# Norm transposes a step later, one exchange first in its queue, three regroupings and one pair of banks reordered

## The chip, the cores and the metric

The kernel runs on one core of a Trainium2 chip. The metric is the device time of one execution in microseconds (us), the median over several executions. Five engines work beside each other, each on its own stream of instructions in the order written: PE (TensorE, matrix products), DVE (VectorE), ACT (ScalarE), POOL (GpSimd) and SP (SyncE), which here issues nearly all DMAs. They wait for each other through semaphores. SBUF is the on-chip memory of 128 partitions; PSUM holds the results of matrix products, in eight banks of 2 KB a partition.

## The reference

One transformer block in float32: self-attention, cross-attention to a context, and a gated feed-forward, each behind a layer norm and with a residual. Batch 2, 1024 rows of 256 features, 16 heads of 64, a context of 154 rows of 192 features, 1024 gated features.

```python
h = _layernorm(x, ln1_g, ln1_b)
x = _attention(h, h, sa_wq, sa_wk, sa_wv, sa_wo, sa_bo) + x
h = _layernorm(x, ln2_g, ln2_b)
x = _attention(h, cond_emb, ca_wq, ca_wk, ca_wv, ca_wo, ca_bo) + x
h = _layernorm(x, ln3_g, ln3_b)
p = h @ ff_w1 + ff_b1
a, gate = (p[..., :D_FF], p[..., D_FF:])
h = a * jax.nn.gelu(gate, approximate=False) @ ff_w2 + ff_b2
return h + x
```

## The kernel before

The order of every instruction is written out by hand; no scheduler changes it. All of it is one stream of Python loops that emit instructions for the five engines, and each engine keeps its own.

**Units and steps.** A unit is a batch row and a pair of heads, 16 in all. Self-attention is a loop over 128 steps `p`, eight a unit (a step's slot is `p % 8`). A step computes the scores of 128 rows against all 1024 keys for the two heads (`s`, L497), their maxima on DVE (L681), the exponents on ACT (L508, output `p`), and an exchange of the running maxima and sums between partitions by four DMAs (`st`, L518). POOL turns these into differences (`dd`, L526 and L527) and denominators (L537 and L539), ACT into factors (`ee`, L532), DVE takes reciprocals (`rd`, L609), POOL scales the exponents by them (L619), and DVE transposes them in 32 by 32 blocks (`pT`, L644). In slots 3 and 4, and 7 and 0, PE does the weighted sums with the values (`po`, L549), which begin in slot 3 or 7 and need the transposed weights of four earlier steps; ACT copies them out in the step after (`store` in `self_values`, L666).

**Work beside.** In the other slots `run_work` puts projections beside the scores, for the next unit (`pq_sa`, `pk_sa`, `pv_sa`), output tiles (`py_sa`, L471, added to `x` at L478) and the layer norm that the next stage needs. What such a piece returns, its store, is emitted in the next step, after that step's scores and maxima and ahead of its exponents (`flush(stores)`):

```python
then = self_first(p)
flush(stores)
then()
```

**The norms beside.** `norm_beside` (L331) lays out a norm in small steps: statistics (`stats`, L240), deviation (L246), normalise (an offset on DVE, L256, then two activations on ACT, L274, or on POOL at L271 in the wide form) and turn (`turn`, L284): four transposes of a 128 by 128 tile by PE into one PSUM bank, `ph_ln`, and as store four activations by ACT into `hT_ln` (L299). In the narrow form, which is self-attention's norm of the second batch row and cross-attention's of the first, one row tile is taken per step and the four turns of each norm come in slot 5 of units 3, 4, 5 and 6, and of 11, 12, 13 and 14. Normalise of a later tile pair comes in slot 6.

**Banks.** `mm_tile`, `sum_tile` and the scores each rotate over two buffers in PSUM. The turn's `ph_ln` and the weighted sums' `po` both take `sum_tile`. A tile that takes a buffer waits until the earlier one there has been read.

**SP's queue.** SP issues in order: the four DMAs of each exchange, the weights ahead of their use (`load_ahead`, `load_weights`, L134, L123), and what stands in the list `later`, among it the swaps of the context's values between partitions (`v_ca`, L800) and the copies of their ends (L805).

**Cross-attention and the gated stage.** Cross-attention has 48 steps `c`, three a unit: scores (`sc`, L828), maxima, exponents (L845), scaling (L856), transposes into the ring `pT_ca` (L872). `cross_regroup` (L889) then copies blocks by eight DMAs between partitions into a single tile of pairs (shown as `wf`, whose memory it uses), and `cross_weigh` lets `cross_values` (L908) make the weighted sums `poc` of a unit in two parts: part 0 in two `sum_tile` banks, part 1 in two `mm_tile` banks, each copied out to `o_ca` (L922). Only when both parts of two units are there can the output tiles `py_ca` be made. The last two units' sums, 14 and 15, lie among the first steps of the gated feed-forward (`pa`, `pb`, `pc`, L1029), whose `pa` also takes `mm_tile` banks; there the copies of a part are shared by ACT and DVE (`pools` is set).

Of the kernel before, what the change touches and what calls it, by code (L numbers as in the profile page):

```python
# [18 lines left out]
def tile_transformer_block(ctx: ExitStack, tc: tile.TileContext, a: dict, out: bass.AP):  # L19
# [11 lines left out]
    HP = NPAIR // NQ  # L31
    NT = S // P
# [20 lines left out]
    SH = GH // 2  # L53
# [44 lines left out]
    for n in names:  # L98
        k = n_of[n]
# [39 lines left out]
    def load_weights(kind, pr, what):  # L139
        if kind == "sa" or what == "q":  # L140
            wsl[kind, pr, what] = load_slice(f"{kind}_w{what}", pr * P, P, HR)
        elif pr % 2 == 0:
            wsl[kind, pr, what] = load_slice(f"{kind}_w{what}", pr * P, VC, CC)
# [23 lines left out]
    for n in names[2:]:  # L167
        own = rows[row_of[n] - n_cols:row_of[n] - n_cols + n_of[n], :]
        p = HR if n in twice else P
# [44 lines left out]
    hT, vs, qk, oT = {}, {}, {}, {}  # L214
# [93 lines left out]
    def tile_order(kind):  # L308

        if kind == "ff":  # L310
            return list(range(NT))
        return [t for i in range(NT // 2) for t in (i, NT // 2 + i)]

    def narrow(kind, b):

        return kind == "sa" or kind == "ca" and b < B - 1

    def add_biases(kind, b):

        bo = {"sa": "sa_bo", "ca": "ca_bo", "ff": "ff_b2"}[kind]  # L320

        def add(t):
            xs = xt[b, t // GT][:, t % GT, :]
            nc.gpsimd.tensor_tensor(xs, xs, bias[bo], ALU.add)

        later.extend(lambda t=t: add(t) for t in range(NT))
        if b == B - 1 and kind != "ff":
            later.append(lambda: load_bias({"sa": "ca_bo", "ca": "ff_b2"}[kind]))

    def norm_beside(kind, b):  # L330

        after = {"sa": None, "ca": "sa", "ff": "ca"}[kind]
        stats, deviation, normalize, turn = norm_pieces(kind, b)
        n = 1 if narrow(kind, b) else 2
        lag = {}
        for fns, first in ((turn, 3), (stats, 0), (deviation, 1), (normalize, 2)):
            for i, fn in enumerate(fns):  # L340
                t = i if fns is stats else 2 * i + 1
                lag.setdefault(first + t // n, []).append((fn, fns is turn))
        for k in range(NT // n + 3):
            tiles = tile_order(kind)[k * n:(k + 1) * n]
            needs = [(after, b, half, t) for half in range(NQ) for t in tiles if after]

            def step(fns=lag[k]):
                done = [fn() for fn, _ in fns]
                return next((fn for fn in done if fn), None)

            side.append((any(turns for _, turns in lag[k]), needs, step))
        if not narrow(kind, b):
            side.append((False, (), lambda: add_biases(kind, b)))

# [203 lines left out]
    side, lates = [], []  # L558
    stores, adds = [], []
    later = []  # L560

    def run(piece):
        done = piece()
        if done is not None:
            (adds if getattr(done, "adds", False) else stores).append(done)
# [34 lines left out]
    SA = 2 * SH * NU  # L600
# [113 lines left out]
    def load_ahead(p):  # L714

        ui, n = divmod(p, 2 * SH)
        for what in "qkv":
            at = {"q": 2, "k": 3, "v": 2 * SH - 1}[what] + 3 * (ui == 0 and what != "v")
            if n != at or ui + 2 >= NU and what == "k":
                continue  # L720
            if ui + 2 < NU:
                load_weights("sa", units[ui + 2][1], what)
            elif ui + 2 == NU or what == "q":
                load_weights("ca", units[ui + 2 - NU][1], what)
        if p == SA - 2:
            load_weights("ca", units[2][1], "q")
        if p in (LAG + 1, 2 * SH - 1, SA - SH - 6):
            load_keys(2 * (1 + (LAG + 1, 2 * SH - 1, SA - SH - 6).index(p)), 2)


    CG = [(t, min(TG, NT - t)) for t in range(0, NT, TG)]
    CA = len(CG) * NU
# [144 lines left out]

    def cross_regroup(c):

        ui, n = divmod(c - len(CG) - 2, len(CG))  # L880
        if n != 0 or not 0 <= ui < NU:
            return
        for a2 in range(2):
            for a4 in range(P // KB):
                half, e = divmod(a4, 2)
                own = slice(a4 * KB, (a4 + 1) * KB)
                src = slice((2 * half + a2) * KB, (2 * half + a2 + 1) * KB)
                blocks = pTc["ring"][src, ui % 3, :2 * NM].rearrange("p (m e) j q -> p m e (j q)", e=2)
                nc.sync.dma_start(  # L889
                    out=pTc["pairs"][own, a2].rearrange("p m j q -> p m (j q)"), in_=blocks[:, :, e])  # L890

    def cross_values(ui, a2):

        b, pr = units[ui]
        v, v0 = vs["ca", b, pr // 2], pr % 2 * P
        if a2 == 0 and pr % HP == 0:
            oT["ca", b, pr // HP] = pt_.tile([P, HP, S], F32, tag="oT", name=f"o_ca{b}_{pr}")  # L900
        quarters = (a2, 2 + a2)
        po = {a4: (mm_tile if a2 else sum_tile)(f"poc_{ui}_{a4}") for a4 in quarters}
        for m in range(NM + 1):
            for a4 in quarters:
                r0 = a4 // 2 * QG
                r = slice(r0, r0 + QG)
                for j in range(2):
                    nc.tensor.matmul(  # L908
                        po[a4][j * DH:(j + 1) * DH, :NT * KB],
                        lhsT=v[r, m + a2 * (m == NM), v0 + j * DH:v0 + (j + 1) * DH],  # L910
                        rhs=pTc["pairs"][r, a2, m, j] if m < NM else
                        pTc["ring"][r, ui % 3, NB - 1, j, :],
                        start=(m == 0), stop=(m == NM),
                        tile_position=(r0, j * DH),
                    )
        dst = oT["ca", b, pr // HP][:, pr % HP, :].rearrange(
            "p (t a q) -> p t a q", a=P // KB, q=KB)

        def store():
            for a4 in quarters:  # L920
                copy = nc.scalar.copy if pools and a4 // 2 else nc.vector.tensor_copy
                copy(dst[:, :, a4, :], po[a4][:, :NT * KB].rearrange("p (t q) -> p t q", q=KB))  # L922

        return store
# [18 lines left out]
    def cross_weigh(c):  # L943

        ui, n = divmod(c - 2 * len(CG) - 1, len(CG))
        if n == 0 and 0 <= ui < NU:
            for part in range(2):
                run(lambda: cross_values(ui, part))
            flush(stores)

# [4 lines left out]
    wsum, wh, ub, psum, pools = {}, {}, {}, {}, {}  # L955
# [259 lines left out]
    with tc.manual_schedule():  # L1215
        stats, deviation, normalize, turn = norm_pieces("sa", 0, True)
# [58 lines left out]
        for p in range(SA):  # L1275
            if p % (2 * SH) == 0:
                self_beside(p // (2 * SH))
            if p == SA - SH:
                work.extend(held)
                held.clear()  # L1280
# [3 lines that stand above are left out]
            turn_group(p - LAG - 1, 1)  # L1284
            turn_group(p - LAG, 0)
            if adds:
                adds.pop(0)()
            flush(kept)
            if later and (p < 4 or p % (2 * SH) in (2, 4, 6)):
                later.pop(0)()  # L1290
            if p in ahead:
                ahead[p]()
            load_ahead(p)
            h, hg = divmod(p, SH)
            ui, n = divmod(p, 2 * SH)
            if h and hg == SH - 1:
                run(lambda: self_values(h - 1, 0))
            elif h > 1 and hg == 0:
                run(lambda: self_values(h - 2, 1))
            else:  # L1300
                run_work(2 if p < SA - SH else 1, h % 2 or h == 0, sum_tile)
                if p == LAG:
                    load_weights("sa", units[1][1], "v")
            if hg == LAG:
                f = (ui - NPAIR // 2 - 1) * EC
                if n == LAG and 0 <= f < DA // 2:
                    load_ends(f, min(EC, DA // 2 - f))
                elif n == SH + LAG and 0 <= f < DA // 2:
                    run(lambda: context_ends(f, min(EC, DA // 2 - f), sum_tile))
                if n == SH + LAG and ui in (0, 1, NU - 1):  # L1310

                    pr = {0: 2, 1: 4, NU - 1: 6}[ui]
                    run(lambda: context_keys(pr, sum_tile))
                    kept.append(context_keys(pr + 1, mm_tile))

        for c in range(CA):
# [13 lines left out]
            ui, n = divmod(c, len(CG))  # L1330
# [81 lines left out]
        for k in range(2 * FU):  # L1412
            c = CA + k
# [17 lines left out]
            while n_left > 0 and sums:  # L1431
                fn, n = sums.pop(0)
# [51 lines left out]
```

## Time and profile before

| what | value |
|---|---|
| median of 3 executions | 1082.0 us (1080.7 to 1082.27) |
| the profiled execution | 1079.84 us |
| its span | 1078.0 us |
| granted PE clock | 1.000 of full speed |
| PE busy | 1062.9 us, 99% |
| DVE busy | 887.4 us, 82% |
| POOL busy | 774.9 us, 72% |
| ACT busy | 645.6 us, 60% |
| DMA moved | 60.84 MB, mean 56 GB/s |

The page gives for each engine how long it was busy, and groups of instructions by line, engine and operation, with tile names as output<-input. The waits by engine tell for each kind of instruction what ended the idle time in front of it. A timeline has a row for neighbouring instructions of one kind: start from the span's start, length, engine, line, operation, tiles, shape, and how many instructions the row merges. SPq is SP issuing DMAs. PE's matmuls overlap each other, so rows overlap a little. The chain of work that ended last is 87% PE.

### The profile page before, as it was taken

To read this page: it belongs to the slowest core of one execution; us is meant where nothing else is said; L and a number is where in the kernel's file an instruction comes from. 1 tells how busy PE (TensorE), PEld (TensorE's weight loads), DVE (VectorE), ACT (ScalarE), POOL (GpSimd) and SP (SyncE) were. 2 spreads that over 40 slices of the span, in tenths; PEclk is the share of its full clock that TensorE was granted. 3 is DMA by queue.
4 is the path that set the end of the run, shared out by engine and by line. 5 is a ranking of instruction groups with operands and counts; after the bars stand their busy time and mean duration, and the time that the engine had idled before them with its cause. 6 is when DMAs were issued, how large, how long until landed. Compare 5 with 4: busy or idle time off the path is not lost.

```text
span 1078.0 us, 46825 instructions
## 1 busy us (share of the span) xinstructions
PE 1062.9 (99%) x19300; PEld 697.1 (65%) x19300; DVE 887.4 (82%) x1327; ACT 645.6 (60%) x2068; POOL 774.9 (72%) x1652
## 2 busy tenths in 40 slices
PE   8999999999999999999999999999999999999998
PEld 6556556556565565565665655566766777788998
DVE  5789999998989989999989889968877877655554
ACT  5766766677666657676776666656566554342231
POOL 2677777778777777777777777766756786499884
PEclk9999999999999999999999999999999999999999
DMA  3222122112111121111111101125775545000000
GB/s 91 65 74 49 43 48 53 43 43 50 32 43 31 33 51 34 39 42 29 39 40 26 43 15 37 24 70 146 183 181 126 116 109 120 7 5 16 21 11 30
DMA packets 104726, 60.84 MB, mean 56 GB/s; under 512 B 32378, under 2 KB 95298, under 8 KB 104514
## 3 DMA queue, kind: packets, MB, share of 16 engines
q1 hardware_dynamic: 103138, 57.07, 22.2%
q8 instruction: 152, 2.49, 0.9%
q10 hardware_dynamic: 1376, 0.79, 0.2%
q14 instruction: 60, 0.49, 0.1%
HBM read 27.91 MB, written 2.10 MB: 28 GB/s over the span
## 4 chain that ended last, share of the span: by engine, by line
PE 87%; POOL 3%; DMA 3%; DVE 3%; SPq 2%; issue 1%; ACT 1%; POOLq 0%; DVEq 0%; ACTq 0%
PE s L497 19%; PE po L549 19%; PE py_sa L471 5%; PE py_ca L471 5%; PE pv_sa L397 5%; PE pk_sa L366 4%; PE pq_sa L366 4%; PE pq_ca L366 4%; PE poc L908 4%; PE pb L1029 4%; PE pq L1168 3%; PE sc L828 3%; PE pa L1029 2%; PE pc L1029 2%; SPq L518 2%; DMA st<-st 2%
## 5 line engine op out<-in xcount | busy, mean ns | idle before, releaser
L619 POOL TENSOR_SCALAR p<-p,rd,ee 128x512 f32<-128x512 f32 x512 | 390.4, 768 | 94.0 <-DVE rd L609 91.8
L508 ACT ACTIVATE p<-s,st 128x512 f32<-128x512 f32 x512 | 345.5, 686 | 169.7 <-DVE st L681 164.0
L681 DVE TENSOR_REDUCE st<-s 128x2 f32<-128x1024 f32 x256 | 308.7, 1207 | 55.4 <-issue 17.2
L644 DVE STREAM_TRANSPOSE pT<-p 128x1024 f32<-128x1024 f32 x256 | 302.9, 1220 | 2.4 <-POOL p L619 2.2
L497 PE MATMUL s<-k_sa,q_sa 64*32 64x512 f32 x4096 | 250.5, 591 | 2.7 <-ACT p L508 2.0
L549 PE MATMUL po<-pT,v_sa 64*32 64x256 f32 x8192 | 235.6, 376 | 0.6 <-DVE pT L644 0.6
L549 PEld LDWEIGHTS po<-pT,v_sa 64*32 64x32 f32 x8192 | 168.9, 106 | 79.5 <-issue 32.3
L845 ACT ACTIVATE p<-sc,neg 128x154 f32<-128x154 f32 x256 | 96.4, 406 | 82.8 <-DVE rden L853 79.2
L497 PEld LDWEIGHTS s<-k_sa,q_sa 64*32 64x32 f32 x4096 | 76.6, 106 | 105.0 <-issue 57.1
L856 POOL TENSOR_SCALAR p<-p,rden 128x154 f32<-128x154 f32 x256 | 96.8, 399 | 56.7 <-DVE rden L853 56.4
L508 ACT ACTIVATION_READ_ACCUMULATOR p<-s,st 128x1 f32 x512 | 103.7, 203 | 0.0
L526 POOL TENSOR_TENSOR dd<-st 128x8 f32<-128x8 f32 x128 | 25.5, 200 | 69.5 <-DMA st<-st 67.9
L397 PEld LDWEIGHTS pv_sa<-sa_wv,hT_ln 64*128 64x128 f32 x1024 | 58.5, 188 | 14.2 <-issue 7.5
L397 PE MATMUL pv_sa<-sa_wv,hT_ln 64*128 64x128 f32 x1024 | 61.7, 275 | 0.0
L471 PE MATMUL py_ca<-ca_wo,o_ca 128*128 128x256 f32 x256 | 60.0, 382 | 0.5 <-DVE o_ca L922 0.5
L366 PE MATMUL pq_ca<-hT_ln,ca_wq 64*64 64x512 f32 (+1 forms) x544 | 59.9, 590 | 0.4 <-DMA ca_wq<-in_L_xattn_ca_wq_dram 0.4
L471 PE MATMUL py_sa<-sa_wo,o_sa 128*128 128x256 f32 x256 | 59.7, 386 | 0.2 <-ACT v_sa L406 0.2
L834 DVE TENSOR_REDUCE neg<-sc 128x6 f32<-128x924 f32 (+1 forms) x48 | 47.9, 998 | 13.8 <-PE sc L828 13.4
L471 PEld LDWEIGHTS py_sa<-sa_wo,o_sa 128*128 128x128 f32 x256 | 47.3, 190 | 18.3 <-issue 6.9
L366 PE MATMUL pq_sa<-hT_ln,sa_wq 64*32 64x512 f32 (+1 forms) x976 | 56.9, 586 | 0.0
L845 ACT ACTIVATION_READ_ACCUMULATOR p<-sc,neg 128x1 f32 x256 | 56.9, 222 | 0.0
L366 PE MATMUL pk_sa<-hT_ln,sa_wk 64*32 64x512 f32 x960 | 55.3, 589 | 0.6 <-ACT q_sa L381 0.6
(145 smaller groups left out, 1479.2 us busy)
## 6 DMA issues: line engine op xcount, KB each, us to landing
wf<-pT_ca SPq DMA_DIRECT2D x128, 128.0 KB, 2.4
st<-st SPq DMA_DIRECT2D x512, 1.0 KB, 1.9
v_sa<-v_sa SPq DMA_DIRECT2D x32, 256.0 KB, 4.3
sa_wq<-in_L_xattn_sa_wq_dram SPq DMA_DIRECT2D x32, 128.0 KB, 3.3
sa_wk<-in_L_xattn_sa_wk_dram SPq DMA_DIRECT2D x32, 128.0 KB, 3.5
sa_wv<-in_L_xattn_sa_wv_dram SPq DMA_DIRECT2D x32, 128.0 KB, 3.4
ca_wq<-in_L_xattn_ca_wq_dram SPq DMA_DIRECT2D x32, 128.0 KB, 3.2
wf<-in_L_xattn_ff_w_dram SPq DMA_DIRECT2D x12, 256.0 KB, 4.3
```

What stands on the lines that cost most here:

```text
L366: nc.tensor.matmul(pq[r][f:f + m, at:at + n], lhsT=wt[own, c, f:f + m], rhs=h[own, c, t0:t0 + n], start=(c == 0), stop=(c == NH - 1), tile ...
L397: nc.tensor.matmul(pv[r][:, i * P:(i + 1) * P], lhsT=h[own, c, i * P:(i + 1) * P], rhs=wt[own, c, :], start=(c == 0), stop=(c == NH - 1), ...
L471: nc.tensor.matmul(py[:, e * D:(e + 1) * D], lhsT=o[:, i, (t + e) * P:(t + e + 1) * P], rhs=wo[kind][:, g * HP + i, :], start=(i == 0), st ...
L497: nc.tensor.matmul(sc[a4 * KB:(a4 + 1) * KB, j, :], lhsT=q[r, c:c + KB], rhs=k[r, h * HB:(h + 1) * HB], start=True, stop=True, tile_positi ...
L508: nc.scalar.activation(pr[:, j, :], sc[:, j, :], AF.Exp, bias=st[:, 0, 0, i, j:j + 1], accum_out=st[:, 0, 1, i, j:j + 1],)
L549: nc.tensor.matmul(po[a2][d:d + KB, :QH // 2], lhsT=v[r, t, e, d:d + KB], rhs=pT[r, d // DH * NK + n, :], start=(t == 0 and e == 0), stop= ...
L619: nc.gpsimd.tensor_scalar(pr[:, j, :], pr[:, j, :], own["rd"][:, c:c + 1], own["ee"][:, 0, c:c + 1], op0=ALU.mult, op1=ALU.mult,)
L644: nc.vector.transpose(halves[h][:, :, c:c + KB], slots[p]["p"][i].rearrange("p j (n k) -> p (j n) k", k=KB))
L681: nc.vector.tensor_reduce(st[:, 0, 0, i, :], sc[i], AX.X, ALU.max, negate=True)
L845: nc.scalar.activation(pr_[:, j, i, :T], sc[:, j, i * T:(i + 1) * T], AF.Exp, bias=neg[:, j, i:i + 1], accum_out=den[:, j, i:i + 1],)
L856: nc.gpsimd.tensor_scalar(pr_[:, j, i, :T], pr_[:, j, i, :T], rden[:, j, i:i + 1], 1.0, op0=ALU.mult, op1=ALU.mult,)
L1029: nc.tensor.matmul(into[:, :BT], lhsT=lhs, rhs=wh[pair][i], start=first, stop=True, skip_group_check=True)
```

## The change

Four edits.

1. In `norm_beside` the turn of a narrow norm comes one step later: slot 6 instead of slot 5, behind that step's scores and ahead of its two output tiles; its store thus moves from slot 6 to slot 7. Everything else of the norm stays. The wide form is as it was.
2. In `load_ahead` the query weights of cross-attention's third unit are issued at step 122 and not at 126, and at step 126 nothing is taken from `later`. So in SP's queue nothing stands between the exchanges of steps 126 and 127; the value swaps that stood there come at the first step of cross-attention.
3. In `cross_regroup` the regroupings of units 13, 14 and 15 are issued one step earlier, which puts unit 13's ahead of the last value swaps and ends.
4. In `cross_weigh`, in the gated stage, part 1 (the `mm_tile` banks) comes ahead of part 0; the output tile is made by whichever comes first.

```diff
-        for fns, first in ((turn, 3), (stats, 0), (deviation, 1), (normalize, 2)):
+        last = 3 + narrow(kind, b)
+        for fns, first in ((turn, last), (stats, 0), (deviation, 1), (normalize, 2)):
             for i, fn in enumerate(fns):
                 t = i if fns is stats else 2 * i + 1
                 lag.setdefault(first + t // n, []).append((fn, fns is turn))
-        for k in range(NT // n + 3):
+        for k in range(NT // n + last):
...
-            def step(fns=lag[k]):
+            fns = lag.get(k, [])
+
+            def step(fns=fns):
...
-        if p == SA - 2:
+        if p == SA - 6:
             load_weights("ca", units[2][1], "q")
...
-        ui, n = divmod(c - len(CG) - 2, len(CG))
+        ui, n = divmod(c - len(CG) - (1 if c > CA - 6 else 2), len(CG))
...
-        if a2 == 0 and pr % HP == 0:
+        if ("ca", b, pr // HP) not in oT:
             oT["ca", b, pr // HP] = pt_.tile([P, HP, S], F32, tag="oT", name=f"o_ca{b}_{pr}")
...
-            for part in range(2):
+            for part in (1, 0) if pools else (0, 1):
                 run(lambda: cross_values(ui, part))
...
-            if later and (p < 4 or p % (2 * SH) in (2, 4, 6)):
+            if later and (p < 4 or p % (2 * SH) in (2, 4, 6) and p != SA - 2):
                 later.pop(0)()
```

## The prediction

> **What bounds the kernel now.** First the page's head and busy times:
>
> ```profile
> span 1078.0 us, 46825 instructions
> PE 1062.9 (99%) x19300; PEld 697.1 (65%) x19300; DVE 887.4 (82%) x1327; ACT 645.6 (60%) x2068; POOL 774.9 (72%) x1652
> ```
>
> PE is busy for 99% of the span. Only what gives PE less work or takes a stall from it gains, and a new stall adds in full unless a later one absorbs it. So I read the waits by engine for PE next:
>
> ```profile
> PE s L497 <- ACT p L508: 2.0, 5, 1.0
> PE poc L908 <- DMA wf<-pT_ca: 0.6, 1, 0.6
> PE po L549 <- DVE pT L644: 0.6, 1, 0.6
> PE pa L1029 <- DVE o_ca L922: 0.5, 1, 0.5
> ```
>
> (Total, number, longest.) Little is left to win: edits 2 to 4 aim at the last three rows. From 97 to 687 us PE idles once, for 0.24 us, so a stall made in self-attention meets nothing that would absorb it. Third, the timelines around one norm turn (unit 3's, one of eight), PE and then ACT; x is the number of instructions merged into a row, brackets give idle time before it:
>
> ```profile
> 175.20 0.66 PE L284 MATMUL ph_ln<-ident,hT_ln 128*128 128x128 f32 x4
> 175.79 1.95 PE L497 MATMUL s<-k_sa,q_sa 64*32 64x512 f32 x32
> 177.66 3.72 PE L471 MATMUL py_sa<-sa_wo,o_sa 128*128 128x256 f32 x16
> 181.32 1.95 PE L497 MATMUL s<-k_sa,q_sa 64*32 64x512 f32 x32
> 183.06 3.66 PE L549 MATMUL po<-pT,v_sa 64*32 64x256 f32 x128
> ```
>
> ```profile
> 175.30 1.07 ACT L406 COPY v_sa<-pv_sa 128x512 f32<-128x512 f32 x2 [0.35 <-PE pv_sa L397]
> 176.26 1.52 ACT L299 ACTIVATE hT_ln<-ph_ln,cols 128x128 f32<-128x128 f32 x4
> ...
> 180.97 0.21 ACT L532 ACTIVATE ee<-dd 128x8 f32<-128x8 f32 x1
> 182.53 1.09 ACT L274 ACTIVATE hT_ln<-x,off_ln,rstd_ln 128x256 f32<-128x256 f32 x2 [1.35 <-DVE off_ln L256]
> 183.83 0.69 ACT L508 ACTIVATE p<-s,st 128x512 f32<-128x512 f32 x1 [0.21 <-DVE st L681]
> ```
>
> The reader should see that before the change the four stores that empty the turn's bank (L299) start early in the step after the turn, at 176.26, and `po` begins only at 183.06: slack of 5 us. ACT then waits 1.35 us for `off_ln` before the next tiles' normalise (L274).
>
> **Edit 1, the turn a step later.** Work on PE stays; the four transposes move behind the next scores, in front of the `py` tiles. The four stores move one step too, and ACT works in the order written: they now stand behind the normalise pair of the next tiles, ahead of the exponents. `ph` takes one of the two `sum_tile` banks, and in the changed program the first matmul into the second bank of the next `po` waits for the last of these stores. Queued behind that matmul on PE is everything: the rest of `po`, then the scores. On ACT, the exponents.
>
> When the stores end: the scores ahead of the moved turn no longer wait for it, so they and the DVE chain behind them (maxima, transposes, `off_ln`) run 175.79 − 175.20 = 0.59 earlier. Unit 3: normalise ends at 182.53 + 1.09 = 183.62, less 0.59 is 183.03; four stores take 1.41 from there (the row's 1.52 less the 0.11 by which an ACT row overlaps the one ahead): 184.44. PE reaches the second bank at 183.06 + 0.11 = 183.17 (two `po` groups of matmuls lie 0.1 to 0.2 apart) and resumes about 0.06 after the release: stall 1.33. The same reading gives 1.34 for unit 4, 1.36 for unit 11 and 1.34 for unit 12. Units 5 and 13 normalise earlier, since ACT comes to it sooner:
>
> ```profile
> 609.52 1.09 ACT L274 ACTIVATE hT_ln<-x,off_ln,rstd_ln 128x256 f32<-128x256 f32 x2 [0.63 <-DVE off_ln L256]
> ```
>
> 609.52 + 1.09 − 0.59 + 1.41 = 611.43 (+0.06) against `po` at 610.76 + 0.11: 0.62 for unit 13. Unit 5's step has the `pe` matmuls in it, which put `po` off to 269.12; 0.2 there, with the `ends` copy behind the stores. Units 6 and 14 have no tile left to normalise, stores go early, 0. Sum 5.37 + 0.62 + 0.2 = 6.2 us. Bounds: if the 0.59 does not come through (DVE or POOL being late for another reason) each of six sites is 0.59 worse, +3.5; if `off_ln` came a further 1.3 earlier the sum would be 0.
>
> What the turn gives: `ph` and `py` use the array in one shape (128*128), so one change of shape goes. From the last `pv` at 175.00 to the first `s` at 175.79 PE spends 0.79, where four transposes at 0.11 need 0.44; the last `s` to first `py` takes 0.51, and `py` spaces 0.22 after. I take 0.19 a site (bounds 0 and 0.35). Where `po` stalls anyway it only moves `po`'s arrival, so it is kept at units 6 and 14: −0.4.
>
> The Trainium skill's Perfetto Trace Analysis, section Matmuls, would have independent matmul groups rotate through different PSUM banks so that emptying one by ACT or DVE overlaps the next group's matmuls. Here the turn and `po` do rotate through two banks, so by the rule alone edit 1 would be worth 8 × −0.19 = −1.5 and the whole sum about −3.8; the rows above say that the emptying instruction is itself held behind another on ACT, and I go by them.
>
> **Edit 2, the last exchange first.** SP's queue at the end of self-attention (the `st` row at 700.11 is the last exchange):
>
> ```profile
> 675.07 2.47 SPq L134 DMA_DIRECT2D ca_wq<-in_L_xattn_ca_wq_dram  x2
> 678.15 18.49 SPq L518 DMA_DIRECT2D st<-st  x16
> 696.74 1.18 SPq L800 DMA_DIRECT2D v_ca<-v_ca  x2
> 697.96 1.99 SPq L134 DMA_DIRECT2D ca_wq<-in_L_xattn_ca_wq_dram  x2
> 700.11 2.48 SPq L518 DMA_DIRECT2D st<-st  x4
> ```
>
> With swaps and weights gone from in front, it issues about 2 us sooner. POOL waits 2.95 for it (to 704.95), the reciprocal, the transposes (end 712.24) and `po` at 712.39 follow, where PE lost 0.58. Next late is PE's own order; the gain is 0.6 (bounds 0 and 0.6). The price: the two weight loads now issue behind the pair at 675.07, so the exchange at 678.15 waits 0.2 to 2.5 (two issues cost 1.3 in an ordinary row, 2.47 in the one shown). Behind it are POOL's differences at 682.56 and DVE's reciprocal at 685.54, whose input was ready at 684.30: slack 1.24. So 0 to +1.2; I take +0.1, nearest the ordinary row. The `v_ca` swaps and `ends`, moved behind the last exchange, are first needed by cross-attention's first weighted sums at 734.6: nothing. The weights' buffer was read by a projection that PE ended at 667.5, so the earlier loads wait for nothing.
>
> **Edit 3, three regroupings earlier.** Only unit 13's was late:
>
> ```profile
> 898.21 0.60 PE L908 MATMUL poc<-wf,v_ca 64*64 64x256 f32 x4
> 899.43 0.86 PE L908 MATMUL poc<-wf,v_ca 64*64 64x256 f32 x10 [0.62 <-DMA wf<-pT_ca]
> ```
>
> After 898.21 the next was due at 898.43 and came at 899.43: 1.0 lost. On SP that regrouping stood behind the last `v_ca` swaps (issued from 887.59, after an ACT copy) and `ends` (to 891.33), and began at 891.43. It now goes ahead of them, when the pairs' tile is read out at about 889.6, and lands some 2 us earlier: −1.0 (bounds 0 and −1.1). The swaps and `ends` then issue from about 895 to 898.4, for units 14 and 15 alone, read at 909.36; regroupings 14 and 15 have slack.
>
> **Edit 4, the `mm` banks first.** Among the gated tiles, `pa` needs a bank that `poc`'s second part held: its copy ran at 912.21 and PE came late at 912.69, where `poc`'s last row ends its issue at 911.9; 0.78 lost. With that part first its copies lie at 910.9 and the wait is gone: −0.8. At its start the part needs `mm` banks which a gelu frees at 909.07, `poc` starts at 909.36: margin 0.3, so the bounds are −0.8 and +0.3. Unit 15's regrouping, whose source tile is now read second, has about 0.8 left.
>
> **Sum.** +6.2 − 0.4 − 0.6 + 0.1 − 1.0 − 0.8 = +3.5 us. The profiled execution took 1079.84 (span 1078.0): 1083.3, or 1.0032 times. On the median of 1082.0, which lies 0.2% above it, 1085.5. A change below 0.2% (2.2 us) can't be told from none.
>
> **Rivals.**
> A. *The stalls are deeper*: the 0.59 does not come through, because the DVE transposes ahead of `off_ln` wait for POOL's scaling rather than for the maxima, +3.5; or edits 2 to 4 uncover the next wait and return their 2.3. For: POOL's scaling is 72% busy and DVE's step is 5.0 of PE's 5.17 us. Against: POOL idles 94 us on DVE's reciprocals. +5.8 to +7.0: about 1088.5.
> B. *The stalls are shallower*: DVE, given PE's stall, catches up, so `off_ln` comes 0.6 earlier from the second site on. Four sites at 0.7, unit 13 none: about +0.5, 1082.5.
> C. *The other side*: `po` does not wait, because `off_ln` is ready when ACT comes to it. It decides from 1.3 us: in the shown ACT rows, an `off_ln` ready as `ee` ends (181.2) puts the stores' end at 183.1, and `po` starts unhindered. Then 8 × −0.19 − 0.6 + 0.1 − 1.0 − 0.8 = −3.8: 1078.2. Against: DVE takes `off_ln` behind two transposes of 1.2 us each, and its order is not changed.
>
> **How the numbers follow.** Forecast 0.62, own range 1084.0 to 1087.0; A 0.15; B 0.12; C 0.11. 1081.5 to 1089.0 holds the forecast, B and most of A, 0.85; below it lies C. Faster by over 0.2% is C, 0.11; same is B and the forecast's edge, 0.13; slower 0.76.
>
> **What the profile after would show.** Edit 1: in the waits of PE a new row, `po` for ACT's hT_ln (L299), six times, 0.2 to 1.4, 5 to 7 us in all; in the timelines of units 3, 4, 11 and 12 the stores directly behind L274 with exponents pushed 0.6 or more. The rows `po` for DVE pT, `poc` for a DMA and `pa` for DVE o_ca gone. Wrong if no such `po` row is there (C), or if rows for `st` grow near 685 (edit 2's price).

## The result, and the profile after

The changed kernel takes 1085.34 us, the median of six executions (1084.07 to 1088.05), against 1080.92 us for the kernel before on the same chip (six executions, 1079.62 to 1082.27): a ratio of 1.0042 with a 95% interval of 1.003 to 1.0055. Measured once more beside other executions of before, it came to 1.0036 (1.0024 to 1.0049). It is slower, by 4 to 4.5 us. The profiled execution took 1085.62 us. Here and below, microseconds that are given with a ratio are worked out from that ratio and the median of before; the difference of the two medians can lie up to 0.7 us from them.

The page's head and the busy times of PE, after:

```profile
span 1083.8 us, 46829 instructions
PE 1065.7 (98%) x19300; PEld 739.5 (68%) x19300; DVE 887.9 (82%) x1327; ACT 643.9 (59%) x2068; POOL 774.7 (71%) x1652
```

The work is the same (19300 matmuls); PE only stands still more often. The waits of PE after say for what (total, times, longest):

```profile
PE po L552 <- ACT hT_ln L299: 5.6, 6, 1.5
PE s L500 <- ACT p L511: 2.2, 5, 1.0
```

The first row is new and is the largest. The three rows that edits 2 to 4 aimed at, `po` for DVE's transposes, `poc` for a DMA and `pa` for DVE's copy, are no longer there, and neither is the one of `py_ca` for DVE's copy.

Around unit 3's turn, PE's timeline after (start, length, what, merged instructions; in brackets the idle time and what ended it):

```profile
175.37 1.95 PE L500 MATMUL s<-k_sa,q_sa 64*32 64x512 f32 x32
177.25 0.66 PE L284 MATMUL ph_ln<-ident,hT_ln 128*128 128x128 f32 x4
177.74 3.62 PE L474 MATMUL py_sa<-sa_wo,o_sa 128*128 128x256 f32 x16
181.29 1.95 PE L500 MATMUL s<-k_sa,q_sa 64*32 64x512 f32 x32
183.03 0.63 PE L552 MATMUL po<-pT,v_sa 64*32 64x256 f32 x8
184.63 3.44 PE L552 MATMUL po<-pT,v_sa 64*32 64x256 f32 x116 [0.97 <-ACT hT_ln L299]
187.71 0.79 PE L500 MATMUL s<-k_sa,q_sa 64*32 64x512 f32 x4
187.90 0.40 PE L552 MATMUL po<-pT,v_sa 64*32 64x256 f32 x4
188.11 1.90 PE L500 MATMUL s<-k_sa,q_sa 64*32 64x512 f32 x28
```

And ACT's over the same time:

```profile
180.54 0.22 ACT L535 ACTIVATE ee<-dd 128x8 f32<-128x8 f32 x1
182.11 1.09 ACT L274 ACTIVATE hT_ln<-x,off_ln,rstd_ln 128x256 f32<-128x256 f32 x2 [1.35 <-DVE off_ln L256]
183.10 1.48 ACT L299 ACTIVATE hT_ln<-ph_ln,cols 128x128 f32<-128x128 f32 x4
184.47 0.69 ACT L511 ACTIVATE p<-s,st 128x512 f32<-128x512 f32 x1
```

`ph_ln` is turned by 177.9, but its bank is read only from 183.10 on, since ACT, in order, first waits 1.35 us for the offset and does the normalise pair. The first few matmuls of `po`, into the other bank, go ahead at 183.03; the next come at 184.63, just behind the stores' end at 184.58.

How much that costs is best seen by laying the two executions over each other: for each step of self-attention, when the last of its score matmuls starts after, less when it does before. Across a turn (from its unit's slot 5 to the next unit's slot 1) this difference grows by 1.41 us in units 3 and 4, 0.49 in unit 5, −0.19 in unit 6, 1.92 and 1.95 in units 11 and 12, 0.70 in unit 13 and −0.20 in unit 14: 7.5 us. The waits' row shows only 5.6, because it counts the gap in front of one instruction. In unit 3 the few matmuls of `po` that slipped ahead fill 0.63 us of the stall (183.03), without PE being any sooner done.

Later the difference shrinks: by 0.63 at the last `po`, by 1.15 at the regrouping of unit 13, by 0.98 among the gated tiles. The rest, about 1 us, is spread over waits that differ between any two executions (of projections for their weights, among others).

### The profile page after: what moved, and what is told of

It is laid out like the page before. It is cut to its first block, busy times and chain, and to the rows that moved or that the text cites. A ratio compares the mean times of both kernels' runs of the same rounds, so it can differ in the third digit from the quotient of the medians.

```text
span 1083.8 us, 46829 instructions
## 1 busy us (share of the span) xinstructions
PE 1065.7 (98%) x19300; PEld 739.5 (68%) x19300; DVE 887.9 (82%) x1327; ACT 643.9 (59%) x2068; POOL 774.7 (71%) x1652
## 4 chain that ended last, share of the span: by engine, by line
PE 78%; POOL 5%; DMA 5%; DVE 4%; SPq 4%; ACT 2%; issue 2%; POOLq 0%; ACTq 0%; DVEq 0%
PE po L552 17%; PE s L500 15%; PE py_ca L474 5%; PE pq_ca L369 5%; PE py_sa L474 4%; PE poc L911 4%; PE pq_sa L369 4%; PE pk_sa L369 4%; PE pb L1032 4%; PE pv_sa L400 4%; PE pq L1171 3%; DMA st<-st 3%; PE sc L831 3%; SPq L521 3%; POOL p L622 2%; PE pa L1032 2%
## 5 line engine op out<-in xcount | busy, mean ns | idle before, releaser
L500 PE MATMUL s<-k_sa,q_sa 64*32 64x512 f32 x4096 | 263.9, 591 | 2.8 <-ACT p L511 2.2
L552 PE MATMUL po<-pT,v_sa 64*32 64x256 f32 x8192 | 246.0, 376 | 5.6 <-ACT hT_ln L299 5.6
L552 PEld LDWEIGHTS po<-pT,v_sa 64*32 64x32 f32 x8192 | 182.5, 106 | 74.6 <-issue 21.6
L500 PEld LDWEIGHTS s<-k_sa,q_sa 64*32 64x32 f32 x4096 | 98.0, 106 | 89.7 <-issue 41.6
L369 PE MATMUL pk_sa<-hT_ln,sa_wk 64*32 64x512 f32 x960 | 57.8, 590 | 0.1
```

The costliest lines, as they stand in the source:

```text
L369: nc.tensor.matmul(pq[r][f:f + m, at:at + n], lhsT=wt[own, c, f:f + m], rhs=h[own, c, t0:t0 + n], start=(c == 0), stop=(c == NH - 1), tile ...
L500: nc.tensor.matmul(sc[a4 * KB:(a4 + 1) * KB, j, :], lhsT=q[r, c:c + KB], rhs=k[r, h * HB:(h + 1) * HB], start=True, stop=True, tile_positi ...
L552: nc.tensor.matmul(po[a2][d:d + KB, :QH // 2], lhsT=v[r, t, e, d:d + KB], rhs=pT[r, d // DH * NK + n, :], start=(t == 0 and e == 0), stop= ...
```

## The experiments

**The turn alone.** Edit 1 and nothing else on the kernel before:

```diff
-        for fns, first in ((turn, 3), (stats, 0), (deviation, 1), (normalize, 2)):
+        last = 3 + narrow(kind, b)
+        for fns, first in ((turn, last), (stats, 0), (deviation, 1), (normalize, 2)):
...
-        for k in range(NT // n + 3):
+        for k in range(NT // n + last):
```

> The kernel before with edit 1 alone. Theory (the turn's four stores stand on ACT behind the normalise pair, and the second bank of the next weighted sums waits for the last of them): six rows of po waiting for ACT's hT_ln, 5.5 us on PE in all, and +6 to +8 us on the time (ratio 1.0055 to 1.0075), since edits 2 to 4 give nothing here. First rival (the stalls are taken up again before self-attention ends): the same six rows and no more than +2 us. Second rival (it is edits 2 to 4 that cost): within 0.2% of before. For units 11 and 12, which lost 0.5 us more than units 3 and 4 in the changed kernel: if that came from exchanges that happened to land late in that one execution, the four stalls are alike here (about 1.0 idle in front of po); if it belongs to the place, units 11 and 12 show about 1.5 again.

Measured: 1086.68 us against 1080.16, ratio 1.0061 (1.0049 to 1.0073), +6.6 us. The new row in the waits of PE:

```profile
PE po L552 <- ACT hT_ln L299: 5.1, 6, 1.4
```

The six stalls stand and nothing takes them up: laid over the execution before, the sites lose 1.41, 1.42, 0.55, −0.19, 1.47, 1.89, 0.70 and −0.20, in all 7.05 us, and the difference at the end of self-attention (7.41) is still 6.84 at DVE's last instruction. Both rivals fall. Unit 11 came down to the size of units 3 and 4 and unit 12 did not; that question stays for a later run.

**Everything but the turn.** Edits 2, 3 and 4:

```diff
-        last = 3 + narrow(kind, b)
-        for fns, first in ((turn, last), (stats, 0), (deviation, 1), (normalize, 2)):
+        for fns, first in ((turn, 3), (stats, 0), (deviation, 1), (normalize, 2)):
```

> The kernel before with edits 2, 3 and 4, the turn left where it was. Theory: no row of po for hT_ln, the rows po for DVE's pT, poc for a DMA and pa for DVE's o_ca gone, and -2.3 to -2.9 us (ratio 0.9973 to 0.9979). Rival (these edits uncover the next wait and give their gain back): within 1 us of before, with new rows between 680 and 930 us.

Measured: 1077.33 us, ratio 0.9975 (0.9966 to 0.9984), −2.7 us: as the theory had it, and none of the three waits is left. But one place got worse in the profiled execution. POOL's wait for the exchange of step 123, and PE's behind it, in the kernel before:

```profile
682.56 0.20 POOL L526 TENSOR_TENSOR dd<-st 128x8 f32<-128x8 f32 x1 [0.42 <-DMA st<-st]
```

```profile
687.15 1.09 PE L497 MATMUL s<-k_sa,q_sa 64*32 64x512 f32 x16 [1.00 <-ACT p L508]
```

and here:

```profile
685.86 0.20 POOL L526 TENSOR_TENSOR dd<-st 128x8 f32<-128x8 f32 x1 [3.28 <-DMA st<-st]
```

```profile
688.58 3.49 PE L497 MATMUL s<-k_sa,q_sa 64*32 64x512 f32 x32 [2.00 <-ACT p L508]
...
695.69 0.66 PE L497 MATMUL s<-k_sa,q_sa 64*32 64x512 f32 x8 [0.24 <-ACT p L508]
```

Before, POOL waited 0.42 there and PE 1.81 in four pieces, the longest 1.00; here PE waits 2.24, the longest 2.00. That is edit 2's price, but not all of it. Laid over the execution before, this stretch loses 1.66 us, not 0.43. Windows of the same run (the column before the last two is the granted clock):

```profile
686.00:688.00 2.00, 0.58 (x3) 0.17 (x1) 0.44 (x3) 1.57 (x6) 1.83 (x6) 1.00 0.02 1
688.00:690.00 2.00, 1.42 (x16) 0.23 (x16) 2.00 (x3) 1.58 (x5) 2.00 (x4) 0.55 0.00 0
690.00:692.00 2.00, 2.00 (x25) 0.23 (x17) 1.94 (x4) 1.20 (x5) 1.83 (x5) 0.60 0.01 1
```

The means of 0.55 and 0.60 come from a clock of 0.50 for 3.4 us: in windows of 0.1 us it falls at 688.2, while PE still waits (until 688.58), and is back at 1.00 at 691.6. The prediction had named the longer wait, as edit 2's price, but nothing of the clock; a run below goes after it.

**The stores ahead of the normalise pair.** The changed kernel, with the two normalise activations of a narrow norm kept back and emitted behind the turn's stores:

```diff
+            late = []
             for i in range(2):
...
-                if not narrow(kind, b) or first and i == 1:
+                if narrow(kind, b) and not first:
+                    late.append(lambda own=own, xs=xs, i=i: nc.scalar.activation(
+                        own, xs, AF.Identity, bias=off[:, i:i + 1], scale=rstd[:, i:i + 1]))
+                elif not narrow(kind, b) or first and i == 1:
...
+            return (lambda: [fn() for fn in late]) if late else None
...
-                return next((fn for fn in done if fn), None)
+                done = [fn for fn in done if fn]
+                return (lambda: [fn() for fn in done][:0]) if done else None
```

> The changed kernel with the normalise pair of a narrow norm emitted behind the turn's stores instead of ahead of them; the transposes, the bank and everything else stay as changed. Theory (the order on ACT is the cause): the po rows of units 3, 4, 11, 12 and 13 vanish, unit 5 keeps up to 0.5 us, because the copy of the context ends is still behind the normalise pair; the time is 3.3 to 4.3 us below the kernel before (ratio 0.9960 to 0.9970). Rival (the later turn costs by itself, through its place ahead of the output tiles or the later exponents): the time stays 2 us or more above the kernel before.

Measured: 1076.16 us, ratio 0.9965 (0.9951 to 0.9979), −3.8 us. ACT around unit 3's turn:

```profile
180.25 0.22 ACT L542 ACTIVATE ee<-dd 128x8 f32<-128x8 f32 x1
180.35 1.52 ACT L305 ACTIVATE hT_ln<-ph_ln,cols 128x128 f32<-128x128 f32 x4
181.82 1.09 ACT L272 ACTIVATE hT_ln<-x,off_ln,rstd_ln 128x256 f32<-128x256 f32 x2
183.50 0.69 ACT L518 ACTIVATE p<-s,st 128x512 f32<-128x512 f32 x1 [0.59 <-DVE st L691]
```

and PE:

```profile
176.95 0.66 PE L290 MATMUL ph_ln<-ident,hT_ln 128*128 128x128 f32 x4
177.44 3.62 PE L481 MATMUL py_sa<-sa_wo,o_sa 128*128 128x256 f32 x16
180.99 1.95 PE L507 MATMUL s<-k_sa,q_sa 64*32 64x512 f32 x32
182.73 3.66 PE L559 MATMUL po<-pT,v_sa 64*32 64x256 f32 x128
```

The stores now fill the time in which ACT used to wait for the offset. The normalise pair follows without a gap, and the bank is read out at 181.8, 0.9 us before `po` comes. Transposes, banks and their place on PE are those of the changed kernel; only the order of six ACT instructions differs, and no `po` row for `hT_ln` remains. Unit 5 keeps a little, as expected: laid over the execution before, it loses 0.05 us where the other seven sites gain 0.19 to 0.20. The rival, that the later turn costs by its place, falls.

**The same on edit 1 alone.**

```diff
+        last = 3 + narrow(kind, b)
+        for fns, first in ((turn, last), (stats, 0), (deviation, 1), (normalize, 2)):
...
+                if narrow(kind, b) and not first:
+                    late.append(lambda own=own, xs=xs, i=i: nc.scalar.activation(
```

> Edit 1 alone, with the normalise pair behind the turn's stores. Theory: what is left of edit 1 is one change of array shape less a site, 0.19 us each, less up to 0.5 at unit 5: -1.0 to -1.5 us (ratio 0.9986 to 0.9991). Rival (no gain in it, the shapes change as often): within 0.4 us of before. Rival (the later turn costs by itself): +2 us or more.

Measured: 1078.09 us, ratio 0.9985 (0.9977 to 0.9994), −1.6 us. Laid over the execution before, each of the eight sites gains: 0.20, 0.19, 0.20, 0.19, 0.19, 0.20, 0.20, 0.20, in all 1.57. Unit 5 loses nothing either, the expected half microsecond there did not come. (This profiled execution, one of the two slowest of eleven, ends level with the execution before, as it lost as much at waits elsewhere; the −1.6 is from the times.) So a later turn by itself costs nothing and gains 0.19 to 0.20 a site, the size that the prediction gave to one change of array shape. That it is the change of shape was not tried apart from the order. The rule of the Trainium skill's Perfetto Trace Analysis, section Matmuls, that rotating banks let the emptying of one overlap the next group, holds in this run, −1.6 us as against the −1.5 that the prediction worked out by it. With the same two banks and another order on ACT it was +6.6.

**Edits 2, 3 and 4, each alone.** The exchange:

```diff
-        if p == SA - 2:
+        if p == SA - 6:
...
-            if later and (p < 4 or p % (2 * SH) in (2, 4, 6)):
+            if later and (p < 4 or p % (2 * SH) in (2, 4, 6) and p != SA - 2):
```

> The kernel before with edit 2 alone. The prediction's terms: -0.6 for the last exchange and 0 to +1.2 for the exchange of step 123, which waits behind four weight issues; taken +0.1. Profiles of the runs with edits 2 to 4 show POOL waiting 3.0 to 3.3 us for that exchange in two executions and 0.9 in one. So theory: -0.6 to +0.2 us, not to be told from no change (ratio 0.9994 to 1.0002), the wait of po for DVE's pT gone, POOL's and DVE's wait near 685 us longer than before. Rival (the exchange of step 123 costs its whole bound): +0.6 us or more.

Measured: 1080.09 us against 1080.29, ratio 0.9994 (0.9985 to 1.0002): not to be told from no change, as expected. The wait of `po` is gone; POOL waited 1.21 for the exchange of step 123 (0.42 before) without PE losing by it. The rival's +0.6 us or more lies outside the interval, which ends at +0.2.

The regroupings:

```diff
-        ui, n = divmod(c - len(CG) - 2, len(CG))
+        ui, n = divmod(c - len(CG) - (1 if c > CA - 6 else 2), len(CG))
```

> The kernel before with edit 3 alone. Theory: the row poc for a DMA near 899 us gone, -1.0 us, kept to the end (ratio 0.9991; on PE's timeline -0.9 to -1.3 between 895 and 906 us). Rival (the swaps and ends that now issue later hold up units 14 and 15): a new wait of poc for a DMA between 905 and 922 us, and nothing gained.

Measured: 1078.44 us, ratio 0.9986 (0.9977 to 0.9995), −1.5 us. SP's queue there:

```profile
889.85 6.38 SPq L889 DMA_DIRECT2D wf<-pT_ca  x8
896.33 1.18 SPq L800 DMA_DIRECT2D v_ca<-v_ca  x2
897.60 2.49 SPq L805 DMA_DIRECT2D v_ca<-ends  x4
900.20 15.02 SPq L889 DMA_DIRECT2D wf<-pT_ca  x16
```

Unit 13's regrouping is first, from 889.85, and the swaps and ends stand behind it; no new wait between 905 and 922.

The banks:

```diff
-            for part in range(2):
+            for part in (1, 0) if pools else (0, 1):
                 run(lambda: cross_values(ui, part))
```

> The kernel before with edit 4 alone. Theory: the row pa for DVE's o_ca near 912.7 us gone, -0.6 to -0.8 us, and in addition about -0.4 at 924 us if the output tile of units 14 and 15 also starts sooner, as in the changed kernel (ratio 0.9989 to 0.9994). Rival (the regrouping of unit 15, which now waits for a read that comes second, lands late, since edit 3 does not help it here): a wait of poc for a DMA near 921 us that takes 0.5 us or more back.

Measured: 1079.27 us, ratio 0.999 (0.9981 to 0.9999), −1.1 us. PE where `pa` used to wait:

```profile
910.43 0.61 PE L908 MATMUL poc<-pT_ca,v_ca 64*64 64x256 f32 x8
910.97 0.70 PE L1029 MATMUL pa<-hT_ln,wf 128*128 128x256 f32 x2
```

`pa` follows 0.54 behind the last row of `poc`; before it was 1.12. Unit 15's regrouping was in time, the rival's wait is not there.

**Weights between two exchanges that have room.** The version with the stores first, with the query weights issued at step 124:

```diff
-        if p == SA - 6:
+        if p == SA - 4:
             load_weights("ca", units[2][1], "q")
```

> The changed kernel with the turn's stores ahead of the normalise pair, and the weights of cross-attention's third unit issued at step 124 instead of 122, where SP waits for ACT in any case. Theory: the exchange of step 123 is no longer late, POOL's wait for it near 682 us is 1 us or less again, and the time is 0 to 0.8 us below that of the version with step 122: 3.8 to 4.8 us below the kernel before (ratio 0.9956 to 0.9965). Rival (a later exchange pays instead): as with step 122 or slower, with POOL waiting for an exchange after 690 us.

Measured: 1075.21 us (1074.65 to 1076.47), ratio 0.9959 (0.9945 to 0.9972): 4.4 us below the kernel before by the ratio (the medians lie 5.1 apart), as the theory had it, and the fastest of all. SP:

```profile
673.85 1.36 SPq L134 DMA_DIRECT2D ca_wq<-in_L_xattn_ca_wq_dram  x2
676.39 7.59 SPq L528 DMA_DIRECT2D st<-st  x8
684.41 1.35 SPq L134 DMA_DIRECT2D ca_wq<-in_L_xattn_ca_wq_dram  x2
686.75 12.23 SPq L528 DMA_DIRECT2D st<-st  x12
```

POOL's wait for the exchange of step 123 is back at 0.50, and PE's longest wait there at 1.02. The version with step 122 had lost 1.4 us at this place in its profile:

```profile
686.95 3.66 PE L507 MATMUL s<-k_sa,q_sa 64*32 64x512 f32 x32 [1.74 <-ACT p L518]
```

PE waited no longer there in all than in the kernel before (1.82 against 1.81), but nearly all of it at once, and the clock was at 0.50 from 686.9 to 690.3. That leaves the 1.4 us to the clock. Against that version (0.9965) the intervals overlap; that step 124 is better is shown by the trace, not by the times.

**The exchange still later, and the same loads where there is room.** The kernel before with edit 2, and four more small loads behind the weights, which nothing reads:

```diff
         if p == SA - 6:
             load_weights("ca", units[2][1], "q")
+            spill = small.tile([P, 2, 4], F32, tag="zz", name="spill")
+            for i in range(4):
+                nc.sync.dma_start(out=spill[:, i // 2, i % 2 * 2:][:, :2], in_=w["ca_wq"][:P, i * 2:(i + 1) * 2])
```

> Edit 2 alone, with four small loads that nothing reads behind the weights of step 122, so that the exchange of step 123 is some 2.5 to 4 us later still. Seen so far: in profiles with edit 2 in which PE waited about 2 us near 688 us (2.00, 1.74, 2.11 at once) the granted clock stood at 0.50 to 0.63 for 3 to 10 us behind that wait, and the execution lost 1.4 to 5 us there; where PE's longest wait there was 1.0, the clock stayed at 1.00. Theory (it is the long wait that costs the clock): PE waits 3 us or more here, the clock falls in nearly every execution (mean clock 0.998 or less), and the time is 4 to 9 us above the kernel before (ratio 1.004 to 1.008). Rival (the clock falls by chance, the wait only costs itself): mean clock 1.000 in most executions, and +2 to +3.5 us.

Measured: 1083.17 us against 1080.19, ratio 1.0024 (1.0015 to 1.0033), +2.6 us; the mean granted clock was 0.997 or 0.998 in each of 11 executions. PE, and its windows:

```profile
684.69 1.13 PE L791 MATMUL pv_ca<-ca_wv,ctxT 96*128 96x256 f32 x4
689.10 3.83 PE L497 MATMUL s<-k_sa,q_sa 64*32 64x512 f32 x32 [3.27 <-ACT p L508]
692.86 3.58 PE L754 MATMUL pk<-ctxT,ca_wk 96*128 96x320 f32 x8
```

```profile
688.00:690.00 2.00, 0.90 (x15) 0.23 (x16) 1.86 (x3) 1.58 (x5) 2.00 (x4) 0.60 0.01 1
690.00:692.00 2.00, 2.00 (x32) 0.23 (x16) 1.94 (x3) 1.72 (x7) 1.83 (x6) 0.50 0.00 0
692.00:694.00 2.00, 2.00 (x18) 0.83 (x3) 2.00 (x4) 0.63 (x2) 1.28 (x3) 0.50 0.03 2
```

In the kernel before the 8 `pk` matmuls took 2.42:

```profile
689.52 2.42 PE L751 MATMUL pk<-ctxT,ca_wk 96*128 96x320 f32 x8
```

Here they take 3.58. The stretch loses 3.95 us, of which PE's longer wait (3.27 against 1.81) is 1.5 and the slower clock the rest, 2.5; with edit 2's gain behind it 3.3 is left. So the clock falls with the wait, in each execution, as the theory had it, and the rival falls; the loss is smaller than the theory's 4 to 9 and lies in the rival's range of +2 to +3.5, so that the time alone would not have told them apart. The same loads and weights at step 124:

```diff
-        if p == SA - 6:
+        if p == SA - 4:
             load_weights("ca", units[2][1], "q")
```

> The same four loads and the weights at step 124 instead, where SP has some 3.9 us to spare. Both theories: the added loads cost less than at step 122. If they fit into the room: within 0.5 us of the kernel with edit 2 alone (ratio 0.9985 to 1.001) and a mean clock of 1.000 in all executions. If the room is too small, POOL's wait for the exchange of step 125 grows above 2 us and the time with it.

Measured: 1079.56 us, ratio 0.9995 (0.9986 to 1.0003), a mean clock of 1.000 in all 11 executions, and no PE wait above 1.02 there. It is not the loads but their place ahead of an exchange that someone waits for.

**The changed kernel once more**, without an edit.

> The changed kernel once more, for a second profile of it and a ratio beside these runs of before. Open is why units 11 and 12 lose 1.9 to 2.1 us each there and units 3 and 4 only 1.4. If the exchanges that POOL waits for in these units come late by chance, another execution shows units 11 and 12 near 1.4 or mixed; if the place decides, both lose 1.9 or more again. The sum of the parts measured alone (turn +6.6, exchange -0.6, regroupings -1.5, banks -1.1) is +3.4 us; with the trace's own terms +4.7. Expected: +3.4 to +5.0 us (ratio 1.0031 to 1.0046).

Measured: 1084.25 us against 1080.07, ratio 1.0036 (1.0024 to 1.0049). Unit 11 in its second profile, and unit 12:

```profile
530.03 1.31 PE L552 MATMUL po<-pT,v_sa 64*32 64x256 f32 x40 [1.01 <-ACT hT_ln L299]
574.21 1.10 PE L552 MATMUL po<-pT,v_sa 64*32 64x256 f32 x32 [0.99 <-ACT hT_ln L299]
```

In the first the same rows had 1.49 and 1.52 idle. Laid over the execution before, units 11 and 12 lose 1.45 and 1.43 this time. So their extra half microsecond is not in the place. It goes with an exchange that comes late: in the first profile POOL waited, for unit 12's,

```profile
561.52 0.20 POOL L529 TENSOR_TENSOR dd<-st 128x8 f32<-128x8 f32 x1 [2.41 <-DMA st<-st]
```

behind which DVE's reciprocal and transposes, and so the offset, were late by as much as the scores had come earlier; in the second profile that wait was 0.23. The same holds over units 11 and 12 of the three profiles with the turn later and the stores behind: the three sites that lost 1.88 to 1.95 had such a wait of 2.10 to 2.41, the three that lost 1.43 to 1.48 none above 0.72. SP's queue of the first profile shows the two weight loads ahead of that exchange issuing in 2.14 us (1.34 in the profile before):

```profile
555.13 3.31 SPq L521 DMA_DIRECT2D st<-st  x4
558.54 2.14 SPq L134 DMA_DIRECT2D sa_wk<-in_L_xattn_sa_wk_dram  x2
560.84 2.48 SPq L521 DMA_DIRECT2D st<-st  x4
```

At the other two late exchanges the pair took 2.40 and 2.22, at the three in time 1.34. Why an issue takes longer at one time than at another was not tried and stays open.

## Why the prediction was right

It forecast 1085.5 us, 1.0032 times a median of 1082.0 for the kernel before, and the way there holds. That it came within 0.2 us of the measured 1085.34 is luck: the median of three executions that it started from was 1.1 us above that of the six (1080.92), and the change of +3.5 was 0.9 below the +4.4 between the medians.

*Edit 1, the mechanism.* Right in each link: the bank, the order on ACT, and the 0.59 by which the DVE chain moves up. For unit 3 the stores' end was worked out as 184.44; it came at 184.58, and that execution was 0.17 late before the turn. Six of eight sites stall, and the two without a normalise pair do not, as said. The run with the stores ahead of the normalise pair takes the cause away and nothing else, and the stall goes.

*Edit 1, the sizes.* The term of 6.2 less 0.4 was too small: 7.5 and 7.05 in the first two profiles, 6.3 in the third, where no exchange is late at units 11 and 12 (1.42, 1.42, 0.28, −0.20, 1.45, 1.43, 0.70, −0.20), and +6.6 by the times of the turn alone. Three causes. Unit 5 was put at 0.2 and cost 0.49 and 0.55 in the first two profiles, since the stores ended 0.2 later than worked out (0.28 in the third). Units 11 and 12 lost the 0.59 when an exchange was late, which is rival A's "does not come through", at two of six sites and in some executions; and behind it stood POOL waiting for a DMA, not POOL's work. And units 3 and 4 cost some 0.1 more than the 1.33 worked out for the stall of the second bank. This fits the split rows of `s` at 187.71 and 188.11: PE's two halves of rows come out of the stall 0.4 apart, and the step ends with the later half. No run tests it.

*The change of shape*, 0.19 a site, was exact in size: 0.19 to 0.20 at all eight.

*Edit 2.* −0.6 + 0.1: the gain showed as 0.63 in the changed kernel and 0.51 with the edit alone. The price was the step with a gap in it. Its bounds, 0 to +1.2, counted the exchange's delay less the slack, and PE's waiting stayed within them; but a long wait costs the clock as well, which no bound held. In the profiles with the weights at step 122 the stretch lost 0 twice (the changed kernel's first, and the exchange alone), 1.4, 1.7 and, in the changed kernel's second, 5.5. Of 40 timed executions with the weights at step 122 and no added loads, 7 have a clock of 0.998 or less, so that the medians carry little of it: −0.6 (−1.6 to +0.2) for the edit alone. Of the 13 timed executions of the changed kernel, the three with a clock of 0.998 or less are its three slowest (1086.52, 1088.05 and 1089.43).

*Edit 3.* −1.0 was put on one wait, and the trace shows −1.15; −1.5 by the times, with the term well inside the interval.

*Edit 4.* −0.8 lacked a part. The wait of `py_ca` for DVE's copy also shortened, by 0.4: the first matmul of that tile now starts at 930.00, ahead of the last copies at 930.10, where before it waited for the last copies. Which of a tile's needs held it, its input or its bank, was not tried apart. −0.98 by the trace.

*The sum.* The stalls were taken too small and so were the gains, which offset each other in part, by luck. The +3.5 that was forecast is near +3.4, the sum of the parts measured each alone (+6.6 − 0.6 − 1.5 − 1.1), and somewhat under the +3.9 to +4.5 measured of the whole, whose intervals hold it.

*The rivals.* A's second branch, that edits 2 to 4 return their gain, fell with the run of them alone (−2.7). The 72% that it gave to POOL's scaling is all of POOL; the scaling (L619) was busy 390.4 us, 36% of the span. C, that `po` does not wait, needed the stores 1.3 us sooner; they came when worked out, and C is what the run with the other ACT order made of it (−3.8, where C said −3.8). B, that DVE catches up, fell (its own terms make +0.3 rather than the +0.5 that it gave): the second site of each norm loses as much as the first.

## What to carry to other kernels

Before a producer into a shared bank is moved later, follow the instruction that empties the bank on its own engine: it moves too, and lands behind whatever that engine does in the new place. Here two activations that waited 1.35 us for a small result of DVE held back a bank by 2.4 us (1.35 of waiting and 1.09 of work), and a turn that was worth −1.6 us cost +6.6; reordering six instructions on an engine that was busy 59% of the time gave all of it back. Where an engine waits for an input, put the work that others wait for in front of the wait. And count a wait of PE near 2 us for more than its length, since the clock may fall in it: the same 1.8 us of waiting cost 1.4 us more at once than in four pieces.

## What was not expected of the hardware

The granted clock follows PE's waits, on this scale: in the four profiles with a wait of 1.74 to 3.27 us, behind four small matmuls, the clock went to 0.50, and the place lost more by that than by the waiting (3.95 us for 1.5 us more waiting, 1.4 us for none). It fell while PE was waiting, and the time at 0.50 came in steps of 3.4 us: 3.4 for the waits of 1.74 and 2.00, 6.8 for 3.27, and 10.2 for 2.11 with another 0.78 close behind. So the length of a wait alone does not tell how long the clock stays down. Waits of 1.02 us at that place, and of 1.5 in front of `po`, left it at 1.00. From the last of the four, the changed kernel's second profile:

```profile
696.00:698.00 2.00, 1.22 (x20) 0.23 (x16) 1.94 (x3) 1.57 (x6) 1.83 (x7) 0.63 0.00 0
...
704.00:706.00 2.00, 2.00 (x32) 0.61 (x24) 0.62 (x1) 0.00 (x0) 0.00 (x0) 0.50 0.06 9
```

The Trainium skill's TensorE: Matmul & The Clock Gate, in its summary Why this matters for your kernels, asks for no idle gap of PE above some 3 us, since an idle window halves the clock. The half is what these rows show. The 3 us are not: 1.74 and 2.00 were enough here.

After unit 3's stall the `s` matmuls, which the kernel puts on the two halves of the array's rows, start 0.4 us apart (187.71 and 188.11), and a gap of 0.97 in the waits stands for 1.6 us from the first `po` at 183.03 to the next at 184.63. And a pair of weight loads of the same size on the same queue took 1.34 us to issue at three places and 2.14 to 2.40 at three others, and each time it took the longer, an exchange came late and, two engines later, a stall on PE was half a microsecond longer.
